# Out-projection of a Mamba-like layer: seven products for eight, partial sums kept in DRAM by accumulating transfers

## The chip, the cores and the metric

The kernel runs on one core of a Trainium2 chip, in float32 throughout. The metric is the device time of one execution in microseconds (us); the runs of one kernel are summed up by their median.

## The reference, cut to what matters

Four layers follow one another, each added to a residual of 1024 tokens x 512 channels: an attention with a linear memory, a mixture of low-rank experts, a state-space layer (Mamba-2-like) and a second mixture. The change sits in the state-space layer, in its last product:

```python
y = Y_diag + Y_off + D_residual            # 256 tokens x 8192 channels, in 4 sequences
var = mean(square(y), axis=-1)
y = y * rsqrt(var + EPS) * norm_w * silu(gate)
return y @ out_proj_w.T                    # (1024 x 8192) @ (8192 x 512)
...
x = x + L1_attn(layernorm(x))
x = x + L1_ffn(layernorm(x))
```

The factor rsqrt(var) is one number per token, so the kernel applies it after the product.

## The kernel before, in words

All code is in one function, `model_kernel`, in two phases, each with its own pools of memory. The first phase (lines 197 to 349) computes the attention and the first mixture. The second (from line 352) does the state-space layer and the second mixture. Where the second phase's pools lie over memory of the first, their first writes wait for the last use there.

**Units.** The state-space layer runs over 72 units (line 581): for each of 8 groups one "bc" unit and 8 "pair" units. A pair is 128 channels (two heads of 64) of the 8192, so there are 64 pairs. Each unit goes through three stages, one unit apart:
- `stage_a` (line 603) projects 512 channels to two tiles of 128 x 1024 tokens (`project`, line 513). It already uses seven products for eight: sums of token blocks (`tok`, line 493) and sums of weight blocks (`weight_sums`, line 503, on GpSimd) replace one product. It yields between groups of products, so that other work can be put in between. PSUM banks with the tag "in" (four of them) take the products, and ScalarE copies some of them away (`keep`, line 531).
- `stage_t` (line 636) transposes, multiplies by the step sizes, and turns the broadcast cumulative sums (`cst`, loaded by `load_sums`, line 624) into decay factors: 16 ScalarE activations (line 701), one exponential (line 705), two VectorE products (line 707).
- `stage_c` (line 712) makes the pair's output `y` (products of lines 721 and 729; VectorE at lines 737 and 740), and adds its square, made by ScalarE at line 739, to `ssq`. The finished tile, 128 channels x 1024 tokens, is appended to `ys`.

**The out-projection.** `out_project(q, t, upto)` (line 756) takes 128 tokens t, and multiplies `ys[j][:, tokens]` by the pair's weights `wouts[j]` (128 x 512) for the pairs j that quarter q has not yet had, four pairs as a rule, summed in one PSUM bank with the tag "mm1" (two banks). VectorE then adds the bank to `acc`, a tile in SBUF of 8 x 128 tokens x 512 (line 771; the first time it copies, line 769). The tokens lie on the partitions. One pair costs eight matmuls of 128x512.

**The loop** (line 818): in each round n it starts `stage_a(n)`, puts half of the out-projection after the first group of products, runs `stage_c(n - 2)` and `stage_t(n - 1)` by `turn`, and puts the other half in between. Each matmul of the source is two instructions in the profile.

**The order of the queues.** The code gives a priority by its order, but a planner puts each engine's instructions, and the DMA issues of SP, in the order in which it expects them to be ready; `issue_after` and a table called `early` fix a few by hand in units 0 to 4. Each engine then works through its queue strictly in order.

**The end** (from line 857): the last pairs' products, the variance over 8192 channels (line 868), then for each 128 tokens `finish(t)`: scale, add the residual that was kept in DRAM (`xr`), layernorm, transposes; then the second mixture with its logits (line 157) and its base product (line 171).

**Time steps** (`time_steps`, line 402): the weights `wdt` of the step sizes and two per-head rows (`dtb`, `na`) are used at the start of the phase only: `ps_dt` (line 412), then a chain on VectorE to `adt` (line 447).

Of the kernel before, what the change touches and what calls it, by code (L numbers as in the profile page):

```python
# [16 lines left out]

# [29 lines left out]
PER_OUT = 4  # L47
# [4 lines left out]
def model_kernel(ctx: ExitStack, tc: tile.TileContext, a: dict, out: bass.AP):  # L52
# [10 lines left out]
    acc = const.tile([P, NT, DM], F32, tag="acc", name="acc")  # L63
# [16 lines left out]
    def toks(t):  # L80
        return slice(t * P, (t + 1) * P)
# [63 lines left out]
    def lora_mixture(name, E, R, w_base, w_cat, w_up, route, psum, pool, done, order=range(NT), ready=None):  # L145
# [6 lines left out]
        for i, t in enumerate(order):  # L152
            if ready:
                ready(i)
            ps = psum.tile([P, 512], F32, tag="mm1", name=f"{name}_psl{t}")
            for k in range(KT):
                nc.tensor.matmul(  # L157
                    ps[:, : E + ER],
                    lhsT=xnT[:, k, toks(t)],
                    rhs=w_cat[:, k, :],  # L160
                    start=(k == 0),
                    stop=(k == KT - 1),
                )
            nc.vector.tensor_copy(lg[:, t, :], ps[:, :E])
            nc.vector.tensor_copy(h[:, t, :ER], ps[:, E : E + ER])
# [186 lines left out]
    with ExitStack() as c1:  # L352
# [17 lines left out]
        wdt = cw.tile([P, KT, P], F32, tag="wdt", name="wdt")  # L370
        nc.sync.dma_start(out=wdt, in_=a["win"][T_DT])
# [12 lines left out]
        f1_up = cw.tile([P, DM], F32, tag="f1_up", name="f1_up")  # L384
        nc.gpsimd.memset(f1_up, 0.0)
        nc.sync.dma_start(out=f1_up[:32, :], in_=a["f1_up"])
# [4 lines left out]
        dtr = cw.tile([P, NB, P], F32, tag="dtr", name="dtr")  # L391
        cs_d = dram.tile([P, (NT + NB) * P], F32, tag="cs_d", name="cs_d")
# [7 lines left out]
        xyp = c1.enter_context(tc.tile_pool(name="xyp", bufs=8))  # L400

        def time_steps():

            dtb = cw.tile([P, P], F32, tag="dtb", name="dtb")
            nc.sync.dma_start(out=dtb, in_=a["dt_bias"].to_broadcast([P, P]))
            na = cw.tile([P, P], F32, tag="na", name="na")
# [305 lines left out]
        def stage_c(n):  # L712
# [25 lines left out]
            sq = bcp.tile([P, NTOK], F32, tag="sq", name=f"sq{j}")  # L738
# [9 lines left out]
        def load_wout(j):  # L748
            if j < NPAIR:
                w = woutp.tile([P, DM], F32, tag="wout", name=f"wout{j}")  # L750
                nc.sync.dma_start(out=w, in_=a["wout"][j])
                wouts[j] = w

        behind = [0] * PER_OUT

        def out_project(q, t, upto):

            j0 = behind[q]
            ps = Psum.tile([P, 512], F32, "mm1", f"ps_p{upto}_{t}")
            for j in range(j0, upto):  # L760
                last["pe"] = nc.tensor.matmul(  # L761
                    ps,
                    lhsT=ys[j][:, toks(t)],
                    rhs=wouts[j],
                    start=(j == j0),
                    stop=(j == upto - 1),
                )
            if j0 == 0:
                nc.vector.tensor_copy(acc[:, t, :], ps)  # L769
            else:  # L770
                nc.vector.tensor_tensor(acc[:, t, :], ps, acc[:, t, :], ALU.add)  # L771
# [6 lines left out]
        for j in range(6):  # L778
            load_wout(j)

# [36 lines left out]
        added = 0  # L817
        for n in range(len(units) + 3):
            a_steps = stage_a(n) if n < len(units) else iter(())
            fresh = [(upto, (upto - 1) % PER_OUT) for upto in range(added + 1, len(ys) + 1)]  # L820
            next(a_steps, None)
            for upto, q in fresh:
                out_project(q, 2 * q, upto)
            turn(n, 0)
            next(a_steps, None)
            turn(n, 1)
            next(a_steps, None)
            for upto, q in fresh:
                out_project(q, 2 * q + 1, upto)
                behind[q] = added = upto  # L830
                load_wout(min(behind) + 5) if upto >= PER_OUT else None
            turn(n, 2)
            next(a_steps, None)
            if n == max(early):
                last["bar"] = None
            if 1 < n < len(units):
                load_sums(n)

# [19 lines left out]
        for k in range(2):  # L858
            nc.sync.dma_start(out=f1_base[k], in_=a["f1_base"][:, 2 * k : 2 * k + 2, :])
        x_v = x_d.rearrange("(t p) d -> p t d", p=P)  # L860
# [12 lines left out]
        order = [2 * PER_OUT - 2, 2 * PER_OUT - 1] + list(range(2 * PER_OUT - 2))  # L873

        def finish(t):
            if behind[t // 2] < NPAIR:
                out_project(t // 2, t, NPAIR)
            x[t] = acc[:, t, :]
            nc.vector.scalar_tensor_tensor(
                x[t], x[t], rs[:, t : t + 1], xr[t // 4][:, t % 4, :], ALU.mult, ALU.add  # L880
            )
            layernorm(t, PsumF, Fin, on_act=True)

        def ready(i):
            for t in order[:3] if i == 0 else order[i + 2 : i + 3]:
                finish(t)
# [8 lines left out]
        lora_mixture("f1", 4, 8, f1_base, f1_cat, f1_up, route_top1, PsumF, Fin, store, order, ready)  # L895
# [57 lines left out]
```

## Time and profile before

| what | value |
|---|---|
| median of 5 runs | 1870.04 us (1869.25 to 1871.82) |
| the profiled execution, its own time | 1871.82 us |
| its span, first to last instruction | 1869.8 us |
| mean granted TensorE clock | 0.993 |
| instructions | 20526 |
| VectorE: acc adds of line 771 | 126 x 686 ns |
| DMA | 180.41 MB, mean 96 GB/s |

In the profile, PE is TensorE's matmuls and PEld its weight loads, DVE is VectorE, ACT ScalarE, POOL GpSimd, SP the engine that issues most DMAs. A group of instructions is written as line, engine, operation, out<-in, shapes, count, then its busy time, the mean duration of one in ns, and the engine's idle time before them with what ended it. Matmuls are pipelined: the duration of one is longer than the interval at which they follow each other. The clock is TensorE's granted share of full speed.

### The profile page before, as it was taken

How to read it: one execution, taken by the hardware profiler on the slowest of the kernel's cores; microseconds unless marked ns; L12 is line 12 of the kernel's file. 1: busy time of each engine (PE TensorE's matmuls, PEld its weight loads, DVE VectorE, ACT ScalarE, POOL GpSimd, SP SyncE). 2: the span in 40 equal slices, each digit the busy share in tenths (PEclk: the TensorE clock that was granted, in tenths of full speed). 3: DMA queues.
4: the chain of work that ended last, by engine and by line, in shares of the span. 5: the costliest groups of instructions: out<-in, count | busy, mean ns of one | idle time of the engine just before them, and what ended most of it. 6: DMA issues, size and time to landing. Idle time of an engine off the chain costs nothing.

```text
span 1869.8 us, 20526 instructions
## 1 busy us (share of the span) xinstructions
PE 1836.4 (98%) x7726; PEld 962.6 (51%) x7726; DVE 1292.6 (69%) x1477; ACT 1066.7 (57%) x1848; POOL 305.9 (16%) x347
## 2 busy tenths in 40 slices
PE   7999989999999999999999999999999999999999
PEld 4645544554555555555555455555555555555554
DVE  4523698876776867776777677777767776866761
ACT  4311259765666656664666566646666666656630
POOL 5210231212111211121112111211112111211000
PEclk9999999999999999999999999999999999999999
DMA  8100133322233232222322222223322223232211
GB/s 321 57 1 12 51 119 122 110 101 68 100 111 112 84 108 101 102 102 85 114 106 102 74 101 102 101 92 111 108 106 68 96 102 106 99 111 102 102 46 45
DMA packets 49058, 180.41 MB, mean 96 GB/s; under 512 B 5984, under 2 KB 7008, under 8 KB 39616
## 3 DMA queue, kind: packets, MB, share of 16 engines
q1 hardware_dynamic: 46848, 167.82, 25.6%
q0 software_dynamic: 1536, 10.24, 1.5%
q8 instruction: 61, 1.00, 0.2%
q10 hardware_dynamic: 576, 1.05, 0.2%
q14 instruction: 37, 0.30, 0.1%
HBM read 174.11 MB, written 4.98 MB: 96 GB/s over the span
## 4 chain that ended last, share of the span: by engine, by line
PE 94%; DVE 2%; ACT 2%; DMA 2%; issue 0%; POOL 0%; ACTq 0%; SPq 0%; DVEq 0%; POOLq 0%
PE pa L522 26%; PE ps_p L761 23%; PE pd L522 13%; PE pb L522 6%; PE ps_y L721 6%; PE f_pso L171 3%; PE ps_q L94 3%; PE ps_o L306 3%; PE ps_xt L679 3%; PE ps_y L729 3%; PE f_psl L157 1%; DMA cst<-cs_d 1%; PE ln_ps L121 1%; PE ps_n L278 1%; PE ps_g L644 1%; PE f_pso L190 1%
## 5 line engine op out<-in xcount | busy, mean ns | idle before, releaser
L761 PE MATMUL ps_p<-wout,xT 128*128 128x512 f32 x1024 | 461.6, 593 | 1.2 <-DVE acc L769 1.2
L701 ACT ACTIVATE cst<-cst,cs 128x128 f32<-128x128 f32 x1024 | 325.1, 392 | 88.7 <-DMA cst<-cs_d 67.9
L761 PEld LDWEIGHTS ps_p<-wout,xT 128*128 128x128 f32 x1024 | 193.8, 190 | 243.7 <-issue 239.8
L507 POOL TENSOR_TENSOR wsum<-win 128x256 f32<-128x256 f32 x72 | 78.4, 1089 | 1265.8 <-PE pa L522 659.8
L565 DVE SCALAR_TENSOR_TENSOR xT<-raw,convw,xT 128x1020 f32<-128x1020 f32 (+2 forms) x216 | 275.1, 1275 | 2.4
L739 ACT ACTIVATE sq<-xT 128x1024 f32<-128x1024 f32 x64 | 67.7, 1057 | 340.3 <-DVE xT L737 340.3
L707 DVE TENSOR_TENSOR cst<-cst,gt 128x1536 f32<-128x1536 f32 x128 | 220.6, 1757 | 46.4 <-ACT cst L705 45.9
L771 DVE TENSOR_TENSOR acc<-ps_p,acc 128x512 f32<-128x512 f32 x126 | 86.4, 686 | 197.1 <-PE ps_p L761 197.1
L705 ACT ACTIVATE cst<-cst 128x3072 f32<-128x3072 f32 x64 | 176.9, 2764 | 0.7
L721 PE MATMUL ps_y<-cst,xdt 128*64 128x128 f32 x2048 | 160.3, 276 | 0.0
L721 PEld LDWEIGHTS ps_y<-cst,xdt 128*64 128x64 f32 x2048 | 119.3, 137 | 50.8 <-issue 48.5
L522 PE MATMUL pa<-xnT,wsum 128*128 128x512 f32 x288 | 141.7, 614 | 0.7 <-ACT keep L533 0.7
L522 PE MATMUL pd<-tok,wsum 128*128 128x512 f32 x288 | 137.1, 593 | 2.5 <-POOL wsum L507 2.5
L522 PE MATMUL pa<-tok,win 128*128 128x512 f32 x288 | 135.8, 594 | 1.6 <-DVE sg L552 1.6
L522 PE MATMUL pa<-xnT,win 128*128 128x512 f32 x288 | 135.9, 592 | 0.2 <-DVE raw L545 0.2
L522 PE MATMUL pa<-tok,wsum 128*128 128x512 f32 x288 | 135.6, 593 | 0.2 <-ACT keep L533 0.2
L522 PE MATMUL pb<-xnT,win 128*128 128x512 f32 x288 | 135.5, 592 | 0.0
L522 PE MATMUL pd<-xnT,wsum 128*128 128x512 f32 x288 | 135.3, 592 | 0.0
L533 ACT COPY keep<-pa 128x512 f32<-128x512 f32 x144 | 83.0, 577 | 65.6 <-PE pa L522 65.6
L545 DVE TENSOR_TENSOR raw<-pb,keep 128x512 f32<-128x512 f32 x72 | 49.6, 688 | 85.1 <-PE pb L522 79.5
L729 PE MATMUL ps_y<-cst,xdr 128*64 128x128 f32 x1024 | 101.9, 273 | 0.0
L573 ACT ACTIVATE xT<-xT 128x1024 f32<-128x1024 f32 x72 | 76.1, 1056 | 33.1 <-DVE xT L565 33.0
(178 smaller groups left out, 2399.4 us busy)
## 6 DMA issues: line engine op xcount, KB each, us to landing
cst<-cs_d SPq DMA_DIRECT2D x64, 1536.0 KB, 6.3
win<-in_win SPq DMA_DIRECT2D x144, 256.0 KB, 2.8
wout<-in_wout SPq DMA_DIRECT2D x64, 256.0 KB, 4.2
wo_s<-in_wo POOLq DMA_DIRECT2D x8, 1024.0 KB, 5.6
wq<-in_wq SPq DMA_DIRECT2D x8, 256.0 KB, 5.1
x_d<-x SPq DMA_DIRECT2D x8, 256.0 KB, 2.0
xr<-x_d SPq DMA_DIRECT2D x2, 1024.0 KB, 5.3
out<-acc SPq DMA_DIRECT2D x8, 256.0 KB, 2.0
```

The source lines that it names most:

```text
L507: op(v[:, 0], w[:, 1, 0:2], w[:, 1, 2:4], ALU.add)
L522: last["pe"] = nc.tensor.matmul(ps, lhsT=wt[:, k, :], rhs=tk[:, k, :], start=start and k == 0, stop=k == 1, skip_group_check=not start,)
L533: nc.scalar.copy(c, ps)
L565: nc.vector.scalar_tensor_tensor(d[:, :, k:], src[:, :, : SEQ - k], convw[:, i, TAPS - 1 - k : TAPS - k], d[:, :, k:], ALU.mult, ALU.add,)
L573: nc.scalar.activation(dst, dst, AF.Silu)
L701: nc.scalar.activation(m[:, hh, c, :], m[:, hh, c, :], AF.Relu, bias=cs[:, c, h : h + 1], scale=1.0)
L705: nc.scalar.activation(mf, mf, AF.Exp, scale=-1.0)
L707: nc.vector.tensor_tensor(mf[:, hh], mf[:, hh], gr.rearrange("p c l -> p (c l)"), ALU.mult)
L721: last["pe"] = nc.tensor.matmul(flat(py)[e, toks(c)], lhsT=xdt[:, c, e], rhs=m[:, hh, c, :], start=True, stop=c % 2 == 0,)
L729: last["pe"] = nc.tensor.matmul(flat(py)[e, toks(c)], lhsT=xdr[:, c // 2, e], rhs=m[:, hh, NT + c // 2, :], start=False, stop=True,)
L761: last["pe"] = nc.tensor.matmul(ps, lhsT=ys[j][:, toks(t)], rhs=wouts[j], start=(j == j0), stop=(j == upto - 1),)
L771: nc.vector.tensor_tensor(acc[:, t, :], ps, acc[:, t, :], ALU.add)
```

## The change

The out-projection is laid out with the 512 output channels on the partitions and the tokens along the free dimension, in 2 x 2 blocks: two halves of 256 output channels, two halves of 512 tokens, and two pairs ("e" and "o") summed over. With sums of weight blocks (`out_weight_sums`, four GpSimd operations of 128x256 for two pairs) and sums of token blocks (`out_token_sums`, four VectorE subtractions of 128x512) seven products take the place of eight. Each product is made for two 128-channel parts m, so two pairs cost 14 matmuls of 128x512.

A product adds two doubles of pairs, `(i - 1, i)`, in one PSUM bank; part m = i mod 2 is done in the rounds of double i, so seven products come up in two rounds, three in the first and four in the second. ScalarE copies a product to a staging tile (three of them), and a DMA on GpSimd's queue adds the tile to `prod_d` in DRAM; the first writes it. There are 210 such transfers of 256 KB. At the end the 14 sums are read back, the last products are added to them from PSUM by VectorE (`add_last`), and `put_together` forms the four blocks of each part m with seven operations. `finish(t)` multiplies the last two pairs in the plain way, adds the four blocks by products with the identity, which turn the channels back to the free dimension, and scales.

```diff
-        behind = [0] * PER_OUT
-        def out_project(q, t, upto):
...
+        def out_weight_sums(i):
+            if 2 * i + 2 < NPAIR:
+                e, o = wouts[2 * i], wouts[2 * i + 1]
+                v = osp.tile([P, 3, 256], F32, tag="osum", name=f"osum{i}")
+                op = nc.gpsimd.tensor_tensor
+                op(v[:, 0], e[:, 256:], o[:, 256:], ALU.add)
+                op(v[:, 1], v[:, 0], e[:, :256], ALU.subtract)
+                op(v[:, 2], o[:, :256], v[:, 1], ALU.subtract)
+                op(e[:, 256:], e[:, :256], e[:, 256:], ALU.subtract)
+                osums[i] = v
+        def out_token_sums(i):
+            e, o = ys[2 * i], ys[2 * i + 1]
+            t = [b2.tile([P, 512], F32, tag=f"ysum{k}", name=f"ysum{i}_{k}") for k in range(3)]
+            sub = lambda r, p, q: nc.vector.tensor_tensor(r, p, q, ALU.subtract)
+            sub(t[0], e[:, 512:], e[:, :512])
+            sub(t[1], o[:, 512:], t[0])
+            sub(t[2], t[1], o[:, :512])
+            sub(e[:, 512:], o[:, 512:], e[:, 512:])
+            ysums[i] = t
...
+        def out_product(m, p, over, bank, to):
+            ps = Psum.tile([P, 512], F32, bank, f"ps_p{over[-1]}_{m}_{p}")
+            for i in over:
+                w, y = out_operands(i, m, p)
+                last["pe"] = nc.tensor.matmul(ps, lhsT=w, rhs=y, start=i == over[0], stop=i == over[-1])
+            to(ps, m, p, over)
+        def add_up(ps, m, p, over):
+            st = osp.tile([P, 512], F32, tag="prod", name=f"prod{over[-1]}_{m}_{p}")
+            nc.scalar.copy(st, ps)
+            first = over[0] == 0
+            nc.gpsimd.dma_start(
+                out=prod_d[m][p // 2][p % 2], in_=st, accum_op=ALU.bypass if first else ALU.add
+            )
+        def load_prods():
+            homes = [bcp.tile([P, 2, 512], F32, tag=f"tok{q}", name=f"out_a{q}") for q in range(3)]
+            homes += [wsp.tile([P, 2, 512], F32, tag="wsum", name=f"out_b{q}") for q in range(2)]
+            homes += [b2.tile([P, 2, 512], F32, tag="raw", name=f"out_c{q}") for q in range(2)]
...
+        def add_last(ps, m, p, over):
+            nc.vector.tensor_tensor(prods[m][p], ps, prods[m][p], ALU.add)
+        def put_together(m):
+            g = prods[m]
...
+        def begin_out(i):
+            out_token_sums(i)
+            for p in ORDER:
+                todo.append((i % 2, p, (i - 1, i) if i else (0,)))
...
+        def end_out(i):
+            if i:
+                load_wout(2 * i + 4)
+                load_wout(2 * i + 5)
+                out_weight_sums(i + 2)
...
-        for n in range(len(units) + 3):
+        for n in range(len(units) + 2):
...
+            bank, to = ("mm1", add_up) if n < len(units) else ("in", add_last)
+            if n == len(units):
+                load_prods()
+            if len(ys) >= 2 * began + 2:
+                begin_out(began)
+                began += 1
+            share = len(todo) // 2 if len(todo) > 4 and n < len(units) else len(todo)
             next(a_steps, None)
+            out_products(2, bank, to)
             turn(n, 0)
             next(a_steps, None)
             turn(n, 1)
             next(a_steps, None)
+            out_products(share - 2, bank, to)
+            if share and not todo:
+                end_out(began - 1)
             turn(n, 2)
...
+            if n == len(units):
+                for p in ORDER:
+                    out_product(1, p, (NPAIR // 2 - 2,), bank, to)
...
+        parts = [put_together(m) for m in range(2)]
         def finish(t):
...
+            ps = Psum.tile([P, 512], F32, "mm1", f"ps_out{t}")
+            for j in (NPAIR - 2, NPAIR - 1):
+                nc.tensor.matmul(
+                    ps, lhsT=ys[j][:, toks(t)], rhs=wouts[j], start=j == NPAIR - 2, stop=j == NPAIR - 1
+                )
+            for d in range(4):
+                part = parts[d % 2][d // 2][t // 4]
+                nc.tensor.matmul(
+                    ps[:, toks(d)], lhsT=part[:, toks(t % 4)], rhs=ident, start=False, stop=True,
+                    skip_group_check=True,
+                )
```

To make room, four things move. `acc` (16 KB per partition) goes. `wdt` becomes a tile of a pool that holds the `sg` tiles (three buffers), and is loaded inside `time_steps`. `dtb` and `na` share one of the six `wout` buffers, which the weights of a pair get afterwards. `f1_up`, used by the second mixture, is loaded at the end, into an `sg` buffer. The square of y (line 739) is written over `xdt` and no longer has a tile of its own. The pool of `xT` tiles has nine buffers for eight. At the end the token blocks go in the order 0 to 7; before, 6 and 7 came first.

## The prediction, made before the changed kernel was built

> **What bounds the kernel now.** I read the page's busy shares first, then the chain of work that ended last, then the table of stages, and last one unit of the steady part in order of time.
>
> ```profile
> PE 1836.4 (98%) x7726; PEld 962.6 (51%) x7726; DVE 1292.6 (69%) x1477; ACT 1066.7 (57%) x1848; POOL 305.9 (16%) x347
> ...
> PE 94%; DVE 2%; ACT 2%; DMA 2%; issue 0%; POOL 0%; ACTq 0%; SPq 0%; DVEq 0%; POOLq 0%
> ...
> L761 PE MATMUL ps_p<-wout,xT 128*128 128x512 f32 x1024 | 461.6, 593 | 1.2 <-DVE acc L769 1.2
> ```
>
> TensorE is busy for 98% of the span and holds 94% of the chain, and the out-projection (L761) waited 1.2 us in all. The table of stages (columns: length, busy time of PE, PEld, DVE, ACT, POOL with instruction counts, granted clock, DMA share, GB/s) shows where the rest is:
>
> ```profile
> 207.00:305.00 98.00, 90.96 (x367) 49.42 (x368) 83.30 (x77) 53.86 (x94) 30.10 (x24) 0.98 0.25 84
> 305.00:1769.20 1464.20, 1461.22 (x6297) 752.52 (x6296) 1075.14 (x1058) 931.87 (x1621) 223.62 (x264) 1.00 0.29 101
> 1769.20:1828.60 59.40, 56.64 (x289) 37.59 (x288) 36.99 (x80) 25.17 (x44) 0.95 (x1) 0.88 0.13 45
> 1828.60:1869.80 41.20, 37.11 (x90) 16.62 (x89) 7.29 (x17) 1.01 (x1) 0.00 (x0) 0.96 0.14 51
> ```
>
> From 305 to 1769 us TensorE has no gaps, at full clock. So a matmul taken out of this stage is worth its whole issue interval, as long as nobody else becomes late. The timeline of TensorE in a steady unit gives that interval:
>
> ```profile
> 1105.00 3.60 PE L761 MATMUL ps_p<-wout,xT 128*128 128x512 f32 x8
> 1108.43 1.04 PE L679 MATMUL ps_xt<-ident,xT 128*128 128x128 f32 x8
> ```
>
> Eight instructions start at 1105.00 and the next group at 1108.43: 0.429 us each. One matmul of the source is two instructions (512 matmuls, x1024), so 0.858 us. A unit is 22.70 us long.
>
> **Steady part: matmuls.** Two channel pairs cost 16 matmuls before and 14 after (seven products by two output halves, the same 128x512 shape). 31 doubles make 434; the last two pairs stay plain, 16 matmuls; and 32 matmuls of 128x128 against the identity are new. Interval of such a small one: ps_dt (L412), 60 instructions in 7.27 us of the chain, 0.121 us; the 128x128 ones of L651 take 0.107. I take 0.114. TensorE: 1024 x 0.429 = 439.3 before; 868 x 0.429 + 32 x 0.429 + 64 x 0.114 = 393.4 after: **45.9 us less**. How it is spread matters: at 1769.2, the end of the last projection, 952 of the 1024 instructions are done; the new order has 413 matmuls (826 instructions) there. So that point moves by 126 x 0.429 = 54.1 us to 1715.1, and the end has more left to do.
>
> **Steady part: the others.** In one unit, 1103.3 to 1126.0, ACT is busy 14.8 us, DVE 16.3 to 17.9, POOL 2.8 to 3.1. The unit becomes about 21.8 us. ACT gets 3.5 copies 128x512 from PSUM (L533: 577 ns), 2.0 us: 16.8 of 21.8. DVE loses two acc adds (L771: 686 ns) and gets on average two subtractions 128x512, half of L743's 1216 ns: 0 net. POOL gets two adds 128x256 (mean of L507 to L510: 0.90) and 3.5 DMA issues (L234: 555 ns): 3.7 more, 6.7 of 21.8. All are hidden under TensorE; the DVE time saved was hidden too and is worth nothing. The longest recurring chain, cst load at 1103.33 to cst multiplied at 1124.5, is needed two units after the load, so it has some 21 us to spare. Copies queue on ACT behind an exponential with its table load (2.76 + 1.28 us), and behind the copies wait the two "mm1" banks; a bank is wanted again 6 us after its product at the earliest. I take 3 us for slips, bounds 0 and 66 (1 us in each of 66 units, the second rival).
>
> **The accumulating transfers** (210 of 256 KB on POOL's queue) have no row. Nearest: x_d<-x, the same bytes from SBUF to DRAM, 2.0 us; from POOL's queue 4.9 to 8.3 us (f_bias, f_base, which queue behind each other). An accumulate also reads DRAM. I take 5 us, bounds 2 and 16 (twice the longest of those rows). Three staging tiles let three be in flight, and 3.5 per 21.8 us are needed, so TensorE notices only above 3/3.5 x 21.8 = 18.7 us each. Bytes: 55 MB written and as many read, beside queue 1's 167.8 MB at 25.6%: some 17% more; cst, win and wout loads have slack. The page "DMA: Bandwidth & Descriptors" of the Trainium skill (Anatomy of one DMA — SWDGE) puts a transfer from this queue at 2.0 us plus its bytes over 436e3; for 262,144 bytes an estimate from that page is 2.6 us, and the sum would be the same. No run here shows an accumulate yet.
>
> **POOL against DVE.** The adds of L507 take 722 ns at least, 1089 on average, and 4810 once, at 264.8 us, just while DVE ran four L565 (two SBUF inputs) end to end. So the two engines do stop each other. The skill's "SBUF — State Buffer" (Who interferes with whom) says the same more strongly: the loser of the shared port blocks for a whole instruction, which speaks against moving 124 more adds to POOL. From rows: 124 x 0.73 = 91 us at most on DVE, 1.4 us in a unit that has 4.8 to 6.4 idle. Nothing on TensorE.
>
> **Start (207 to 305 us).** wdt was loaded at 204.15, ps_dt began at 207.57. Its new buffer lies in a later pool, over memory that the phase before reads until its last transposes (209.3). Then it lands at 209.3 + 3.1 and ps_dt is up to 4.8 us later, with the whole time-step chain; the first unit's products that need no sums (3.4 us) can fill in. Bounds 0 and 4.8, I take 3. The per-head tile holds one of six wout buffers until adt (L447, ends 249.3), so the sixth wout load waits until then. If SP's order puts it before the third unit's win loads (issued 232.86), that unit's first product (242.27) comes 10.6 us late (249.3 + 2.8 to land + 0.73 for the sum). The six wout loads run at 10 us now, far ahead of their place in the code, so SP's order goes by readiness: I take 0.
>
> **The end.** Let T be the end of the last projection. TensorE then has: seven products of two matmuls 12.0, two stage_c 5.5, transposes 0.9, seven single matmuls 6.0, variance 1.7, sixteen plain matmuls 13.7, identity matmuls 7.3, layernorm transposes 3.5, logits (L157) 6.5: 57.1 us, against 49.0 before; then the last stage of 41.2. Before, 59.4 were taken for 49.0. After: the last stage_c ends at T + 24.4. Then y (1.27, L737), its square (1.06), L740 (1.28), L743 (1.22) and hand-overs of 0.5: T + 29.7. put_together is 14 DVE operations of 0.63 on 128x512; the first seven fit earlier, of the second some 3.3 us are left: T + 33. TensorE has only 5.1 us to do in that time. From there 27.6 us of work, 3 for the last layernorm's chain (L879 to its transposes 3.5 to 4.5 us, less two logits) and 3 for the lower clock after the gap (0.88 in this stage now): T + 66.6, and 107.8 with the last stage, against 100.6 before. Reading the sums back (14 x 256 KB, 11 us at the 321 GB/s of the first slice) starts with the tiles that the last unit frees early; I hide it, bound +12 when it is all late.
>
> **Sum.** 1715.1 + 107.8 + 3 (start) + 3 (slips) = 1828.9 us of span, beside 1869.8. The profiled execution took 1871.82, 2.0 more than its span; the median is 1.8 below it. So **1829 us**.
>
> **Rivals.**
> 1. *The end eats more* (12%): sums read back late (+12) and put_together whole in the path (+5): 1846. For: DVE has 36 us of work in 33. Against: half of the tiles are free 10 to 18 us before T.
> 2. *PSUM banks wait for ACT* (5%): copies sit behind ACT's batches, 1 us lost per unit: 1829 + 63 = 1892; the sign turns at 0.6 us per unit. Against: ACT's 7.9 us of idle per unit.
> 3. *Transfers too slow* (8%): the accumulate holds its staging tile over 18.7 us; ACT, then the bank, then TensorE wait for it. At 20 us a unit is 20 x 3.5/3 = 23.3 us, 1.5 more in some 60 units: 1919. It ends slower than before above about 19.3 us. For: a read and a write of DRAM in each, and no row. Against: 2.0 and 5.6 us (1 MB on the same queue).
> 4. *Doesn't do what it says* (3%): queues are ordered so that the products bunch and only half of the 54 us comes: 1856.
> The forecast has 72%, by itself 1813 (no slips, no loss at the start, full clock, and the 3.5 us of idle at T + 30 and the last chain's 3 filled) to 1845 (SP's order at 10.6, and 5 more of slips).
>
> The range of 1813 to 1862 takes in the first and fourth. Faster by over 0.2% (what a measurement here can tell from no change) 0.85, within 0.02, slower 0.13.
>
> **What would show it.** Right: L761's successors take 868 instructions at 0.429 us, PE without gaps from 305 to some 1715, the accumulates at 2 to 10 us, POOL near 540 us, ACT near 1190. Wrong: idle of PE released by the ACT copy of the products, or ACT idle released by the transfers' landing; a gap of over 10 us near T + 25; a late ps_dt that delays everything after it.

## The result, and the profile after

The changed kernel takes 1874.46 us in the median (29 runs, 1868.63 to 1882.95), the kernel before 1870.49 us (50 runs beside them). The ratio is 1.0022, with a 95% interval of 1.0015 to 1.0029: **slightly slower**, by 0.2%, where 1829 us, in a range of 1813 to 1862, and "faster" were forecast. The profiled execution has a span of 1871.9 us.

The page of after (busy shares, then the chain by engine), and from the groups the row that stands where L761 stood:

```profile
PE 1802.9 (96%) x7666; PEld 945.7 (51%) x7666; DVE 1373.8 (73%) x1495; ACT 1166.2 (62%) x2059; POOL 692.6 (37%) x681
...
PE 65%; ACT 15%; DVE 12%; DMA 4%; issue 4%; SPq 0%; POOL 0%; ACTq 0%; DVEq 0%; POOLq 0%
...
L804 PE MATMUL ps_p<-xT,wout 128*128 128x512 f32 x372 | 172.2, 595 | 1.4 <-DVE xT L744 1.4
```

TensorE really has less to do: 1802.9 us busy, 33.5 less (45.9 were forecast; where the rest went is told below). But it holds only 65% of the chain of waits; before it was 94%. The rest passed to ACT and DVE. The table of stages of after (columns as before) shows where TensorE now stands still:

```profile
320.00:1050.00 730.00, 715.51 (x3108) 368.09 (x3107) 581.79 (x542) 531.38 (x941) 306.79 (x300) 1.00 0.54 140
1050.00:1758.70 708.70, 698.55 (x3064) 360.11 (x3063) 552.19 (x513) 498.70 (x889) 294.54 (x288) 1.00 0.57 143
1758.70:1871.90 113.20, 101.15 (x443) 59.62 (x441) 60.76 (x119) 27.62 (x46) 1.57 (x3) 0.94 0.20 63
```

From 320 to 1758.7 us 24.6 us are idle, at full clock; before, 1461.22 of 1464.20 us were busy. Marks in TensorE's timeline divide the span. The first is the first product of a "bc" unit's second stage (ps_g), which comes once in each group of nine units; T is the end of the last projection.

| stretch | before, us | after, us | change forecast | change measured |
|---|---|---|---|---|
| start to the first ps_g | 267.56 | 282.52 | +3 | +15.0 |
| to the second ps_g | 167.14 | 165.71 | -7.7 (18 instructions x 0.429) | -1.4 |
| six whole groups | 1180.68 | 1159.93 | -41.2 (6 x 16 x 0.429) | -20.8 |
| to T | 153.82 | 150.54 | -5.1 (12 x 0.429) | -3.3 |
| slips, anywhere | | | +3 | in the rows above |
| T to the last instruction | 100.6 | 113.2 | +7.2 | +12.6 |
| span | 1869.8 | 1871.9 | -40.8 | +2.1 |

So three things need an explanation: 12 us at the start, 25.5 in the steady part (the three middle rows give 25.5 where 54.0 were to come; of the 28.5 lost, 3 had been allowed), and 5.4 at the end.

**The start.** ScalarE's timeline of after (start, duration, instruction; in brackets the idle time before it and what ended it), then TensorE's beside it:

```profile
22.49 0.31 ACT L412 ACTIVATE per_head<-per_head 128x128 f32<-128x128 f32 x1 [5.76 <-DMA per_head<-in_A_log]
22.70 0.80 ACT L117 ACTIVATE xn<-x,ln_sh,ln_rs 128x512 f32<-128x512 f32 x1
```
```profile
23.56 1.11 PE L122 MATMUL ln_ps<-ident,xn 128*128 128x128 f32 x4 [4.95 <-ACT xn L117]
```

L412 is the exponential of `na`, which is needed 230 us later. Its new tile, one of the `wout` buffers, is free from the beginning, so the planner put the exponential among the layernorms of the first phase. There it waits 5.76 us for its load, and the last layernorm, queued behind it, runs at 22.70 instead of 16.57. The end of the first phase moves from 201.67 to 210.03 (start of the last product of L191): +8.4. Then ps_dt begins 13.5 us later than before (221.06 against 207.57), 5.1 more: wdt is loaded only at 217.2.

**The steady part.** What TensorE waited for (engine, line, awaited; us in all, times, longest):

```profile
PE pa L526 <- DVE sg L556: 12.2, 8, 2.8
PE pa L526 <- ACT keep L537: 7.8, 7, 1.9
...
PE pd L526 <- POOL wsum L511: 4.5, 2, 3.7
...
PE ps_xt L683 <- DVE xT L741: 3.0, 7, 0.7
```

Seven or eight times each is once per group (ps_xt and the first are neighbours); before, the first two stood at 1.6 and 0.9 us. (The third line, GpSimd's `wsum`, belongs to the first group alone.) In the group change whose bc unit begins at 985.66, TensorE's timeline has these waits and no others:

```profile
958.68 1.09 PE L683 MATMUL ps_xt<-ident,xT 128*128 128x128 f32 x8 [0.59 <-DVE xT L741]
...
962.83 1.98 PE L526 MATMUL pa<-tok,win 128*128 128x512 f32 x4 [1.33 <-DVE sg L556]
...
1024.18 1.98 PE L526 MATMUL pa<-xnT,wsum 128*128 128x512 f32 x4 [1.51 <-ACT keep L537]
```

Together 3.4 us, which is what the group is too long. Behind the first two stands this piece of VectorE's timeline, two rounds ahead of the bc unit:

```profile
943.72 1.21 DVE L777 TENSOR_TENSOR ysum<-xT,ysum 128x512 f32<-128x512 f32 x1
944.86 1.73 DVE L569 SCALAR_TENSOR_TENSOR xT<-raw,convw,xT 128x1012 f32<-128x1012 f32 x1
946.51 1.21 DVE L777 TENSOR_TENSOR ysum<-ysum,xT 128x512 f32<-128x512 f32 x1
947.65 1.21 DVE L777 TENSOR_TENSOR xT<-xT,xT 128x512 f32<-128x512 f32 x1
...
952.56 3.42 DVE L711 TENSOR_TENSOR cst<-cst,gt 128x1536 f32<-128x1536 f32 x2 [3.10 <-ACT cst L709]
```

In this round everything meets: the convolution, three of the four token sums, and on GpSimd eight adds end to end from 940.54 to 950.20 (four of `out_weight_sums`, four of `weight_sums`). A token sum that can take 0.68 us takes 1.21, a convolution's product that can take 1.27 takes 1.73. ScalarE's silu (L577) waits 1.17 us for the convolution, its exponential follows at 949.76, VectorE's products with it at 952.56, and then VectorE works without a pause to the sum that pa waits for (L556, 962.09). The third wait comes from ScalarE: cst lands at 1009.57, after 2.12 us of idle, and the exponential with its table load, a second table load and the second silu of the bc unit stand ahead of keep (1023.56).

Over the whole span the rows of VectorE and GpSimd show the same:

```profile
L569 DVE SCALAR_TENSOR_TENSOR xT<-raw,convw,xT 128x1020 f32<-128x1020 f32 (+2 forms) x216 | 301.6, 1397 | 1.6
...
L777 DVE TENSOR_TENSOR ysum<-ysum,xT 128x512 f32<-128x512 f32 x31 | 35.5, 1144 | 0.0
```
```profile
L811 POOL DMA_DIRECT2D prod_d<-prod x210 | 177.7, 922 | 527.0 <-ACT prod L809 511.2 <-ACT xT L577 11.8 <-issue 3.5
L511 POOL TENSOR_TENSOR wsum<-win 128x256 f32<-128x256 f32 x72 | 96.2, 1337 | 351.0 <-DMA win<-in_win 293.5 <-PE ps_p L804 53.1 <-PE ln_ps L122 4.2
```

L569 took 1275 ns on average before, L511 (then L507) 1089. VectorE has 81 us more in all, where I had put 0; GpSimd has 692.6, where I had put 540.

**The end.** TensorE's timeline of after behind the last `stage_c`:

```profile
1783.92 0.48 PE L733 MATMUL ps_y<-cst,xdr 128*64 128x128 f32 x3
1789.32 3.18 PE L972 MATMUL ps_var<-ones,ssq 128*128 128x1 f32 x16 [4.92 <-DVE ssq L747]
1792.36 3.76 PE L982 MATMUL ps_out<-wout,xT 128*128 128x512 f32 x4
1795.91 0.64 PE L987 MATMUL ps_out<-ident,out_a 128*128 128x128 f32 x2
```

A gap of 4.92 us, and then half speed: four instructions of 128x512 take 3.76 us, elsewhere 1.88, and the granted clock is 0.54 from 1789.3 to 1795.9. The variance stands first in the queue, and the products that need no variance wait behind it. The first product with the identity comes at T + 37.2, where I had T + 33.

### The profile page after: what moved, and what is told of

Read it like the earlier page. It is cut to its first block, busy times and chain, and to the rows that moved or that the text cites. A ratio compares the mean times of both kernels' runs of the same rounds, so it can differ in the third digit from the quotient of the medians.

```text
span 1871.9 us, 21313 instructions
## 1 busy us (share of the span) xinstructions
PE 1802.9 (96%) x7666; PEld 945.7 (51%) x7666; DVE 1373.8 (73%) x1495; ACT 1166.2 (62%) x2059; POOL 692.6 (37%) x681
## 3 DMA queue, kind: packets, MB, share of 16 engines
HBM read 177.78 MB, written 60.03 MB: 127 GB/s over the span
## 4 chain that ended last, share of the span: by engine, by line
PE 65%; ACT 15%; DVE 12%; DMA 4%; issue 4%; SPq 0%; POOL 0%; ACTq 0%; DVEq 0%; POOLq 0%
PE pa L526 17%; PE ps_p L804 14%; PE pd L526 8%; ACT cst L705 4%; ACT cst L709 4%; PE ps_y L725 4%; PE pb L526 4%; PE f_pso L172 3%; PE ps_o L307 3%; DMA cst<-cs_d 3%; PE ps_q L95 3%; DVE xT L569 2%; PE ps_xt L683 2%; DVE cst L711 2%; PE ps_y L733 2%
## 5 line engine op out<-in xcount | busy, mean ns | idle before, releaser
L811 POOL DMA_DIRECT2D prod_d<-prod x210 | 177.7, 922 | 527.0 <-ACT prod L809 511.2
L705 ACT ACTIVATE cst<-cst,cs 128x128 f32<-128x128 f32 x1024 | 326.8, 395 | 26.1 <-DMA cst<-cs_d 25.7
L711 DVE TENSOR_TENSOR cst<-cst,gt 128x1536 f32<-128x1536 f32 x128 | 232.0, 1837 | 113.3 <-ACT cst L709 113.3
L569 DVE SCALAR_TENSOR_TENSOR xT<-raw,convw,xT 128x1020 f32<-128x1020 f32 (+2 forms) x216 | 301.6, 1397 | 1.6
L511 POOL TENSOR_TENSOR wsum<-win 128x256 f32<-128x256 f32 x72 | 96.2, 1337 | 351.0 <-DMA win<-in_win 293.5
L743 ACT ACTIVATE xdt<-xT 128x1024 f32<-128x1024 f32 x64 | 67.7, 1058 | 253.8 <-DVE xT L741 253.8
L804 PE MATMUL ps_p<-xT,wout 128*128 128x512 f32 x372 | 172.2, 595 | 1.4 <-DVE xT L744 1.4
L526 PE MATMUL pa<-tok,win 128*128 128x512 f32 x288 | 137.0, 598 | 12.3 <-DVE sg L556 12.2
L549 DVE TENSOR_TENSOR raw<-pb,keep 128x512 f32<-128x512 f32 x72 | 49.4, 685 | 119.2 <-PE pb L526 109.5
L809 ACT COPY prod<-ps_p 128x512 f32<-128x512 f32 x210 | 117.7, 575 | 25.7 <-PE ps_p L804 20.0
L804 PEld LDWEIGHTS ps_p<-xT,wout 128*128 128x128 f32 x372 | 69.9, 190 | 87.8 <-issue 83.9
L804 PE MATMUL ps_p<-ysum,osum 128*128 128x512 f32 x248 | 112.1, 592 | 0.0
```

The costliest lines, as they stand in the source:

```text
L511: op(v[:, 0], w[:, 1, 0:2], w[:, 1, 2:4], ALU.add)
L526: last["pe"] = nc.tensor.matmul(ps, lhsT=wt[:, k, :], rhs=tk[:, k, :], start=start and k == 0, stop=k == 1, skip_group_check=not start,)
L569: nc.vector.scalar_tensor_tensor(d[:, :, k:], src[:, :, : SEQ - k], convw[:, i, TAPS - 1 - k : TAPS - k], d[:, :, k:], ALU.mult, ALU.add,)
L705: nc.scalar.activation(m[:, hh, c, :], m[:, hh, c, :], AF.Relu, bias=cs[:, c, h : h + 1], scale=1.0)
L711: nc.vector.tensor_tensor(mf[:, hh], mf[:, hh], gr.rearrange("p c l -> p (c l)"), ALU.mult)
L743: nc.scalar.activation(sq, y, AF.Square)
```

## The experiments

Unless it says otherwise, an experiment changes the kernel after in one place. "Group" is the mean of the six whole groups: 196.78 us before, 193.32 after, 189.9 forecast. Ratios are to the kernel before, with 95% intervals.

### The exponential of na

```diff
+            with issue_after(stored[-1]):   # the first phase's last store of x
                 nc.sync.dma_start(out=dtb, ...)
                 nc.sync.dma_start(out=na, ...)
```

> The changed kernel with one edit: the loads of the two per-head rows are issued after the first phase's last store, so that their exponential on ACT can no longer be queued ahead of the last layernorm of the first phase. Theory (ACT waits 5.8 us for the A_log load at 16.7 us and the first phase ends 8.4 us later, 210.0 for 201.7): the first phase ends near 202 again and the time falls by 8 to 9 us to about 1866. Rival (the first phase is late because more loads run in its first 20 us; the exponential only happens to wait there): the phase ends near 208 to 210 and the time stays at 1872 to 1875.

1865.1 us, ratio 0.9971 (0.9961 to 0.9982), 9.4 us less than after. The first phase's last product starts at 199.02 (2.65 us earlier than before the change, which the theory didn't have and no run explains), the time-step products (ps_dt) at 210.10. The exponential was the cause, and the group (194.2) is no better for it.

### wdt in a buffer that is free early

On top of that, `wdt` takes a `wout` buffer in place of an `sg` buffer.

```diff
-            wdt = b3.tile([P, KT, P], F32, tag="sg", name="wdt")
+            wdt = woutp.tile([P, KT, P], F32, tag="wout", name="wdt")
```

> The same edit, and the step-size weights wdt in one of the six wout buffers, which is free from the start, so that they no longer wait for memory of the first phase. Theory (the late wdt, 5.0 us, and the chain after it, about 4 us, are paid in full): another 5 to 9 us less than the first edit alone, 1857 to 1861. Rival (the first units' own chain of sums and cst loads sets the pace there anyway): no more than 2 us less, about 1864 to 1866; a second rival, that the wout buffer lost for 220 us delays the third double's weights, would give a PE wait for osum in the third double and more time.

1858.53 us, ratio 0.9939 (0.9924 to 0.9954), 6.6 us less again. ps_dt starts at 200.68, the first ps_g at 262.00. The two moves of small tiles account for 16 us of the time and for all of the late start: the first ps_g is now 5.6 us earlier than before the change.

### The copies on VectorE

```diff
-            nc.scalar.copy(st, ps)
+            nc.vector.tensor_copy(st, ps)
```

> The changed kernel with the 210 copies of products on DVE in place of ACT. A group of nine units takes 193.4 us, where eight matmuls less would give 189.8; about 25 us are lost over seven groups. Theory ACT (the copies stand in ACT's queue ahead of the keep copies that TensorE waits for): the group falls to 190 to 191 and the time to about 1855. Rival DVE (DVE is late because GpSimd's adds hold it up; PE waits for sg, L556): DVE gets 2.4 us more per unit, the group grows to 195 or more and the time to 1885 or more. Rival transfers (cst lands later): group and time unchanged within 4 us.

1882.37 us, ratio 1.0058 (1.0041 to 1.0075), group 195.35. A wait of this kernel:

```profile
PE ps_xt L683 <- DVE xT L741: 12.4, 9, 1.9
```

It was 3.0 us in after, and pa waits 14.2 for DVE sg. VectorE has no room for the copies: the group is as the rival DVE had it, the time 2.6 us below its 1885. They are best where they are.

### No transfers

```diff
-            nc.gpsimd.dma_start(out=prod_d..., in_=st, accum_op=...)
+            if first:
+                nc.gpsimd.dma_start(out=prod_d..., in_=st)
```

> The changed kernel without the 196 accumulating transfers (the sums are left out; only the first 14 transfers are written, so the output lacks most of the product). Copies and POOL's adds stay. Theory transfers (they lengthen the cst loads, 6.3 to nearly 8 us at the group ends, and their issue on POOL, 922 ns each, delays the weight sums): the group falls to 190 to 191 and the time to about 1850. Rival ACT copies or rival DVE against POOL's adds: group 192.5 to 193.5, time 1870 to 1874 (less only for the last transfers at the end, 2 to 4 us).

1864.7 us, ratio 0.9969 (0.9957 to 0.9981): the transfers cost some 10 us. The group is 192.30, so neither answer fits as it was put. The waits of pa for ACT keep fall from 7.8 to 2.7 us, those for DVE sg stay at 11.9: the transfers own the third of the three waits of a group, not the first two. The way leads over cst: at the group change shown above, the cst load issued at 1000.69 took 8.9 us to land; its counterpart without transfers, issued at 998.78, took 6.3, ScalarE then had no idle time in front of L705, and the wait for keep was 0.32 us for 1.51. ScalarE's idle time for cst is 7.4 us in all, 25.7 in after. That idle time is no price by itself, though: before the change it was 67.9 us, with 0.9 us of waiting for keep.

### No weight sums on GpSimd

```diff
-                op(v[:, 0], e[:, 256:], o[:, 256:], ALU.add)
-                ...
-                osums[i] = v
+                osums[i] = osums["v"]   # made once
```

> Leaves out the out-projection's sums of weight blocks on GpSimd (124 adds of 128x256; three are made once, so that the products read something). Everything else stays. Theory: GpSimd's adds slow VectorE's two-input operations (L569 takes 1397 ns on average beside 1275 before, the token sums 0.83 to 1.14 us each beside some 0.63), and VectorE is then late at the ends of the groups. Then VectorE's busy time falls from 1374 us to 1330 or less, the group of nine units from 193.3 us to 191.5 or less, the waits of pa for the DVE sum from 12.2 us to under 6, and the time from 1874.5 to 1850 to 1862. Rival, VectorE is late by the amount of its own work and the order of its queue, whoever runs beside it: the group stays within 0.5 us of 193.3, the time within 5 us of 1874. Rival, DMA: the same, unchanged.

1861.09 us, ratio 0.9934 (0.9913 to 0.9955). VectorE's rows in this kernel, with exactly the same operations as in after:

```profile
L569 DVE SCALAR_TENSOR_TENSOR xT<-raw,convw,xT 128x1020 f32<-128x1020 f32 (+2 forms) x216 | 284.5, 1318 | 1.6
...
L777 DVE TENSOR_TENSOR ysum<-ysum,xT 128x512 f32<-128x512 f32 x31 | 25.4, 820 | 0.0
```

VectorE's busy time falls by 60 us to 1313.6 without one of its operations being taken away, and pa waits 4.1 us for DVE sg instead of 12.2. The wait two rounds ahead of the bc unit falls from 1.3 us in each group to between 0 and 1.1; the one on keep stays (8.6 us in all). The theory's numbers hold but one: the group, 192.19, misses the 191.5 that I set. About half of the gain lies ahead of the first ps_g (275.50 instead of 282.52); why, no run separates.

### Stores from SP, and plain writes from GpSimd

```diff
-            nc.gpsimd.dma_start(out=prod_d..., in_=st, accum_op=...)
+            nc.sync.dma_start(out=prod_d..., in_=st)      # first kernel
+            nc.gpsimd.dma_start(out=prod_d..., in_=st)    # second kernel
```

> The 210 transfers become plain stores on SP's queue, so the sums over the pairs are left out (each store overwrites the one before). Same bytes written, no reading back of DRAM by the accumulate, no DMA issue on GpSimd (178 us of its busy time). Without nearly all the transfers the kernel took 1864.7. If it was GpSimd's time for the issues or the accumulate that cost those 10 us: 1862 to 1868. If it was the bytes written: 1872 to 1877. Against both stands that a store on SP waits for its ACT copy in order, ahead of the loads of win, cst and wout behind it: then the waits of PE for ACT keep and ACT xT grow above the 12 us of after and the time goes above 1880.

> The 210 transfers stay on GpSimd's queue but write instead of adding, so the sums over the pairs are left out. Takes away the accumulate alone. If the accumulate (a read of DRAM beside the write) costs the 10 us that leaving out the transfers brought: 1863 to 1868, transfers at 3 us or less for 4.5. If the issue on GpSimd costs it: within 3 us of 1874, and the issue's mean stays near 922 ns.

From SP: 1869.48 us, ratio 0.9993 (0.9980 to 1.0006), group 192.73. Plain from GpSimd: 1868.11, ratio 0.9981 (0.9971 to 0.9990), group 192.66. Each lies between the two answers, or at their edge: by the ratios 5.4 and 7.7 us of the 9.9 go with the accumulate. The rest stays with the bytes or the issuing, which these two don't separate further; the interval of the plain writes overlaps that of no transfers. With plain writes pa waits 2.9 us for ACT keep and ScalarE 9.2 for cst, nearly as without transfers: the third wait of a group belongs to the accumulate. What SP's order was to cost didn't appear. The queue and the transfer in the second kernel, and in after:

```profile
q0 software_dynamic: 18336, 65.30, 9.2%
...
prod_d<-prod POOLq DMA_DIRECT2D x210, 256.0 KB, 2.6
```
```profile
q0 software_dynamic: 30880, 65.30, 21.8%
...
prod_d<-prod POOLq DMA_DIRECT2D x210, 256.0 KB, 4.5
```

(Columns: packets, MB, share of 16 engines; then us from issue to landing.) With the accumulate, the same bytes take 64 packets more per accumulating transfer (12544 for 196), 12.6 points more of all the DMA engines' time, and 1.9 us longer. GpSimd's issue takes 922 ns with it and 549 without.

### No token sums on VectorE

```diff
         def out_token_sums(i):
+            if i:
+                ysums[i] = ysums[0]
+                return
```

> Leaves out the out-projection's sums of token blocks on VectorE except for the first double (120 of 124 subtractions of 128x512, 117 us of VectorE busy time; later products read the first double's sums). If VectorE is what is late in the steady part, by its amount of work: the waits of pa for DVE sg go from 12.2 to under 3, the group from 193.3 to 190 or 191, T from 1758.7 to some 1740, the time to 1850 to 1860. If it is the conv and decay products of the bc units alone that bunch, whatever the token sums: group within 0.7 of 193.3, time above 1868.

1861.88 us, ratio 0.9938 (0.9918 to 0.9958), group 192.02; T is 1749.0, where 1740 was foreseen, and pa still waits 6.2 us for DVE sg. Neither answer holds in full: VectorE's amount of work matters, but it is not the only thing.

### The end filled

On the kernel with na and wdt early:

```diff
+        for t in range(4):
+            start_out(t)     # ps_out: ys[NPAIR - 2] by its weights, start=True, stop=False
-        pv = Psum.tile([P, 512], F32, "mm1", "ps_var")
+        pv = Psum.tile([P, 512], F32, "in", "ps_var")
```

> Built on the kernel with na and wdt early (1858.5 us; end, from the last projection product to the last instruction, 113.2). At the end, the product of the last pair but one with its weights is put ahead of the variance for the first four token blocks, so that TensorE has 3.4 us of work in the 4.9 us in which it waits for ssq. Theory: the end was 5 us longer than foreseen because nothing was put into that gap and because the clock was half after it. Then 3.4 us of work move into the gap and the variance (3.2 for some 1.7 us) and the first plain products (3.8 for 1.9) run at full clock: the end takes 106 to 108, the time is 1851 to 1854. Rival: VectorE's put_together, whose last operation ends 37.5 us after T, sets the time of everything behind it; then the end stays at 112 or more and the time at 1857 to 1860.

1854.58 us, ratio 0.9912 (0.9895 to 0.9928). The same place in TensorE's timeline:

```profile
1767.06 2.84 PE L977 MATMUL ps_out<-wout,xT 128*128 128x512 f32 x6
1770.92 1.12 PE L999 MATMUL ps_out<-wout,xT 128*128 128x512 f32 x2 [1.01 <-DVE xT L747]
...
1772.32 1.84 PE L986 MATMUL ps_var<-ones,ssq 128*128 128x1 f32 x16
```

The gap is 1.01 us, the granted clock stays at 1.00 (1766 to 1780), the variance takes 1.84 us instead of 3.18, and the end takes 1847.3 - 1740.6 = 106.7 us. The order of the queue was the cause, not `put_together`. (The end is 6.5 us shorter in the profiled execution, which is the fastest of its four; the medians of four runs each are 4 us apart.)

### Token sums of the bc rounds on GpSimd

```diff
-                begin_out(began)
+                begin_out(began, nc.gpsimd if bc else nc.vector)
```

> Built on the same kernel (1858.5 us, group 193.8, pa waiting 11.1 us for DVE sg). In the rounds that begin a bc unit, where VectorE has two convolutions, the four token sums are made by GpSimd (32 subtractions in all). Theory: VectorE is late for the projection just in these rounds; without 4 x 1 us there the waits of pa for DVE sg fall under 5 us, the group to 192.6 or less, the time to 1847 to 1853. Rival: GpSimd takes 1.3 us or more for each and slows VectorE beside it, and the products then wait for GpSimd: waits of ps_p for POOL appear, the time is 1857 or more.

1856.15 us, ratio 0.9918 (0.9903 to 0.9933), beside 1858.53 without it, which the intervals don't tell apart. Neither answer: pa waits 11.0 us for DVE sg as before (11.1), the group is 193.2, and no wait of ps_p for POOL stands out. The rounds were the wrong ones: the wait lies two rounds ahead of the bc unit, which I saw only afterwards. And with 28 operations less VectorE is busy for 1364.0 us, as long as without the edit (1363.9): what was moved away came back as longer operations beside GpSimd.

### The first tap on ScalarE

```diff
-            nc.vector.tensor_scalar(d, src, convw..., convb..., ALU.mult, ALU.add)
+            nc.scalar.activation(dst, raw, AF.Identity, bias=convb..., scale=convw...)
```

> Built on the same kernel (1858.5 us). The first tap of each convolution (80 operations of 128x1024, 817 ns each on VectorE, 65 us) goes to ScalarE as a scaled copy with a bias. If it is the amount of VectorE's work that is late (120 token sums left out, 117 us, brought 12.6 us of time), 65 us less bring about 7: 1849 to 1853, with pa waiting under 7 us for DVE sg. Rival: the tap then stands in ScalarE's queue behind a batch of activations, VectorE waits for it and TensorE for ScalarE's copies: waits on ACT xT and ACT keep grow past 15 us and the time is 1860 or more.

1850.67 us, ratio 0.9882 (0.9850 to 0.9915), on the same base. VectorE falls to 1309.6 us, ScalarE rises to 1261.6. The time is the one foreseen, the wait is only in part: pa waits 8.6 us for DVE sg, and 12.5 for ACT keep (7.0 before). Some of the lateness has moved to ScalarE, and the group (193.2) is hardly shorter. The gain is mostly in the first group, 162.5 us long instead of 168.1.

### Both improvements

> Both improvements together, on the kernel with na and wdt early: the first tap of the convolutions on ScalarE (alone 1850.7 us) and the last pair but one ahead of the variance (the end 106.8 instead of 113.2). If they add up: T as with the tap alone, 1734 to 1737, the end 106 to 108, the time 1843 to 1847. If the end now waits for ScalarE or VectorE instead: end over 110, time 1850 or more.

1849.42 us (six runs, 1838.45 to 1855.05), ratio 0.9881 (0.9859 to 0.9903). The end takes 105.2 us, a little less than foreseen, but T is 1741.1, 7 us later than with the tap alone. Of these, 4 are there at the first ps_g already (266.58 for 262.42), and pa waits 16.3 us for ACT keep, 12.5 with the tap alone; why, with an edit that touches only the end, isn't shown. The version is 1.2% faster than the kernel before and faster than the one after, but not measurably better than the tap alone.

### All three left out

The kernel with na and wdt early, without the transfers, the weight sums and the token sums.

> The kernel with na and wdt early, and the transfers (after the first 14), the weight sums of the out-projection on GpSimd and the token sums on VectorE (after the first of each) all left out together; the products and the ScalarE copies stay. If these three are the whole of the 26 us lost in the steady part, TensorE runs as the prediction worked it out: a group takes 189.9 to 190.5 us, T is 1709.6 (1769.2 less 54.1, less the 5.5 that this kernel starts its first unit earlier than the one before the change) to 1714, and with an end of 113 the time is 1825 to 1829. Rival: something else of the change, the ACT copies and the banks they hold, or the conv work at the ends of the groups, costs as well: the group takes 191 us or more, T 1718 or later, the time 1833 or more.

1837.11 us, ratio 0.9816 (0.9802 to 0.9831). One whole group of before, of after and of this kernel:

```profile
434.70:631.35 196.65, 196.65 (x845) 101.28 (x844) 143.01 (x142) 123.51 (x215) 29.67 (x36) 1.00 0.28 99
```
```profile
448.23:641.72 193.49, 190.21 (x830) 98.08 (x829) 148.70 (x143) 137.08 (x244) 83.47 (x79) 1.00 0.56 140
```
```profile
620.66:810.84 190.18, 189.87 (x830) 98.24 (x829) 135.33 (x126) 136.97 (x243) 35.67 (x36) 1.00 0.30 103
```

TensorE's work per group is close to what the prediction said, 189.9 us, in both kernels of the new layout (190.2 to 190.8 us busy in the six groups of after, 189.9 to 190.2 in those of this kernel). After needs 193.5 us for the group shown, this kernel 190.2 (mean of six 190.4), and it still has all of ScalarE's copies (137 us in both). So the three together are the loss in the whole groups, and the copies have next to no share: pa waits 2.6 us for ACT keep in all. The three alone shorten the group by 1.0, 1.1 and 1.3 us, together 3.3 on a base of 193.8: they add up. T, 1720.9, and the time are beyond what I set, since the first group stays at 167.0 us and the end takes 114.6.

## Why the prediction was wrong

**TensorE's work: right.** 868 instructions at 0.429 us; the busy time of a group confirms it (six groups: 37.6 us less, 41.2 forecast). Over the whole span only 33.5 of the 45.9 us appear, because the start and the first group ran at a lower granted clock: up to the first ps_g 0.96 for 0.98 and 4.8 us busier, in the first group 0.97 for 1.00.

**The steady slips: the step that failed most.** It read "All are hidden under TensorE", on the strength of one unit from 1103.3 to 1126.0 and its neighbours, with 4.8 to 6.4 us of VectorE idle. I took 3 us, with a bound of 66. Measured are 28.5 us (6.3 of them in the first group, see below), and in the whole groups they lie in two rounds of nine that I hadn't looked at. Idle time in the unit was no cover there: at 949 us VectorE itself waits 3.10 us for ScalarE, which waited for VectorE. A chain that crosses between the two engines is lengthened by each slower step, though both have idle time. Two terms were mis-sized. The net load of VectorE is not 0: the token sums take 121 us, not 75 (124 times half of 1216 ns), and the convolutions 26 us more. And the weight sums on GpSimd are not "nothing on TensorE": without them VectorE is 60 us less busy. The priced bound of 91 us held, the cover over it did not.

**The second rival** (banks wait for ACT) has a similar symptom, an eighth of its size (7.8 us for 63), and a wrong cause: keep is late, not the copies of products; most of it goes away when the accumulates go (7.8 to 2.9 us), as cst then lands earlier.

**The transfers: the size was right, the conclusion was not.** 4.5 us for the 5 taken; the threshold of 18.7 us is far away. Yet they cost 10 us, because they delay other loads (cst 8.9 us for 6.3 at the group change, win 3.9 for 2.8 in the median) and not their own staging tiles. The term that the prediction had put at nothing was "cst, win and wout loads have slack".

**The start: a step was missing.** wdt came 5.1 us later (3 taken, upper bound 4.8). I had asked what the per-head tile holds up behind it, not what becomes early by it: the free buffer let an exponential slip into another phase's queue. That is 8.4 us on TensorE, and no line of the diff shows it.

**The end: half.** 113.2 us, not 107.8; +12.6 for +7.2. The read-back did hide, and the gap near T + 25 was foreseen. That the planner would put the variance at the head of it, so that nothing fills it and the clock halves behind it, was not: the 3 us for the clock became some 5, an estimate from the granted clock (0.54 over 6.6 us, then 0.94 over 34.8).

**The first group** gained 1.4 us of 7.7. Before, TensorE was busy for 159.63 of its 167.14 us, so this stretch did have gaps, and fewer matmuls there only made more of them: 9.3 us for 7.5 (156.43 busy of 165.71). The other 4.5 us lost are busy time at a lower clock. The longest gap, TensorE's line and GpSimd's beside it, and the same place in TensorE's timeline before:

```profile
330.09 3.78 PE L526 MATMUL pd<-tok,wsum 128*128 128x512 f32 x4 [3.72 <-POOL wsum L511]
```
```profile
329.03 1.01 POOL L511 TENSOR_TENSOR wsum<-win 128x256 f32<-128x256 f32 x1 [25.80 <-DMA win<-in_win]
```
```profile
315.26 1.12 PE L522 MATMUL pd<-tok,wsum 128*128 128x512 f32 x2 [0.87 <-POOL wsum L507]
```

The weight sum starts 46.5 us after the first ps_g, 46.2 before the change; TensorE, with less to do, reaches its product earlier, waits 3.72 us for 0.87, and then has a granted clock of 0.52 from 330 to 336. (The length of a gap alone doesn't tell what follows it: after 3.03 us of idle at 288.33 the clock is 0.63 up to 292.4, while before, after 3.54 us at 273.88, it was 1.00 up to 278.) In the runs with a short first group (162.2 us with the copies on VectorE, 162.5 with the tap on ScalarE, 159.3 with both improvements) TensorE waits 0.9 us or not at all for GpSimd's sums; in all the others of the new layout, also with all three loads out (167.0), 4.5 to 4.8 us. No run changed this wait alone.

What stays open is also how the 10 us of the transfers divide between bytes and issuing once the accumulate is gone, and why the runs of after spread over 14 us and those with the tap on ScalarE over 15, where the 50 runs of before spread over 8.

## What to carry to other kernels

Take the cover for added work from the most loaded round of the whole period, not from a typical one, and follow the chain between engines there: idle time that an engine spends waiting for another is no cover. Work that is moved to an engine beside a critical one must be charged with the lengthening of that one's operations, too. When a tile gets a buffer that is free earlier, look for what can now be queued early, and in front of whom.

## What the runs showed of the hardware

**VectorE and GpSimd lengthen each other.** Around 1013 us in after, GpSimd's timeline and then VectorE's:

```profile
1012.88 1.70 POOL L513 TENSOR_TENSOR wsum<-win 128x256 f32<-128x256 f32 x1
1014.53 1.70 POOL L512 TENSOR_TENSOR wsum<-wsum,win 128x256 f32<-128x256 f32 x1
```
```profile
1011.05 1.27 DVE L569 SCALAR_TENSOR_TENSOR sg<-raw,convw,sg 128x1020 f32<-128x1020 f32 x1
1012.24 1.74 DVE L569 SCALAR_TENSOR_TENSOR xT<-raw,convw,xT 128x1012 f32<-128x1012 f32 x1
...
1015.57 1.21 DVE L777 TENSOR_TENSOR ysum<-xT 128x512 f32<-128x512 f32 x1
```

Alone, the convolution's product takes 1.27 us, a token sum 0.68, GpSimd's add some 0.73. Side by side they take 1.74, 1.21 and 1.70. An operation with one input in PSUM isn't lengthened: L549 takes 675 to 693 ns in all its 72 places, one of them at 948.78, beside the eight adds of GpSimd told of above. The Trainium skill ("SBUF — State Buffer", Who interferes with whom) says that VectorE with two SBUF inputs contends with a GpSimd operation that reads SBUF; the rows agree. It also says that the later one blocks until the other is done; in these rows VectorE lost some 0.5 us each time, less than a whole add of GpSimd.

**The accumulate's price.** A plain 256 KB write from GpSimd's queue landed in 2.6 us, from SP's in 2.0, an accumulating one in 4.5. The profile's count of bytes read from DRAM is the same for the accumulating and the plain kernel (177.78 MB), so that the accumulate's reading shows in the packets only, if at all. The skill's fit for this queue ("DMA: Bandwidth & Descriptors", Anatomy of one DMA — SWDGE) gives, as an estimate, 2.6 us: right for the plain write; for the accumulate the measurement decides.
